# Second quartic factor of a Newton step: two matmuls of 128 columns for m and y against one of 256 columns on a joined tile

## The chip, the core and the metric

The kernel runs on one core of one Trainium2 chip. The metric is the device time of one execution in microseconds (us). A core has five engines that run side by side, each with its own queue of instructions: TensorE (PE in the profile, its weight loads PEld), VectorE (DVE), ScalarE (ACT), GpSimd (POOL) and SyncE (SP, which only issues DMA transfers here). They wait for each other through semaphores. Matmul results land in PSUM, which the kernel uses as eight banks of 128 x 512 f32; everything else lives in SBUF or in DRAM.

## The reference

The input x is 32 batches of 32 channels of 128 x 128, f32. Two layers follow, each a residual on a group normalisation.

```
# layer 0: x = x + sqrtm(_gn(x))
normA = sqrt(sum(A2 * A2));  Y = A2 / normA;  Z = I
for _ in range(5):
    T = 0.5 * (3 I - Z @ Y);  Y = Y @ T;  Z = T @ Z
sA = Y * sqrt(normA)

# layer 1: x = x + spectral_conv(_gn(x))
x_dht = real(fft2(x))
top = einsum('bixy,ioxy->boxy', x_dht[:, :, :32, :32], weights1)
bot = einsum('bixy,ioxy->boxy', x_dht[:, :, -32:, :32], weights2)
y = real(ifft2(zeros with top and bot put in their corners))
```

Layer 0 is the heavy one: for each of 1024 channels, five coupled Newton-Schulz steps on a 128 x 128 matrix. Layer 1 keeps 64 x 32 frequencies of each channel, mixes the channels there and transforms back.

## The kernel before

A group is four channels (tiles of 128 x 4 x 128, one PSUM bank). Layer 0 of a group is the generator newton (L400). It folds the five Newton steps into two quartic factors and a last product. quartic (L364) makes v from mb and m, then w from the transpose of v plus r, then q from v and w. With the first q, newton makes y = q m / MS (L404) and the next m = MS q y (L406), both copied out of PSUM by ScalarE through taken (L271, the copy is L276). The transpose of m gives mb (L408) and r (L409). With the second q, L412 makes two products: pw = q m and py = q y. pw is copied as one 128 x 512 to a tile called "t" (L413, name w in the code); py is copied channel by channel, scaled by that channel's norm sn (L416, tile "y4"). products(w, q) (L418) follows, then products(t, y) is added to the input (L420).

products (L304) takes one PSUM bank and issues four matmuls of 128 columns, one per channel. All matmuls of layer 0 have L307 in the profile; their tiles tell them apart: "m,q" is pw, "y,q" is both py and the product of L406, "q,t" is products(w, q). The transposes are L313. In profile names a group's m in the first quartic is "x".

Batches 1 to 18 are "far": for them v's transpose goes by VectorE and two DMAs on SyncE's queue through DRAM (L373 to L386), and GpSimd adds r (L388). The other batches ("near") transpose on TensorE.

The order of work is written by hand as lanes (L997 on). Up to nine groups are in progress. In each round every lane runs one step; each yield from rest ends two steps, so the parts of a group lie two rounds apart, and other groups' instructions stand between them in each queue. A new group starts every three (far) or five (near) rounds. The same loop weaves in layer 1: folding on GpSimd (L433), forward transforms (L455, L461, L467), spectra (L523), channel mixing (wide_products L608, small_products L678, last_products L723), and the inverse (L859, L881, with copies at L893 and unfolding at L898 and L827). The tile framework then places the semaphores and may move an instruction within its engine's queue; DMAs and some activations are pinned to program order (kept).

Rooms (L259) says how many places each kind of tile has: the first number in a pool that stays, the second in a pool that is freed when the early stage ends. y and m have (4, 2) each. In the tail, weights (L747) loads the last channel-mixing weights on SyncE's queue into rooms that Newton no longer needs: kinds lists which kind may be taken after how many steps of the last group.

Of the kernel before, what the change touches and what calls it, by code (L numbers as in the profile page):

```python
# [29 lines left out]
F32 = mybir.dt.float32  # L30
# [6 lines left out]
P = 128  # L37
# [13 lines left out]
MS = -QA * QS  # L51
# [17 lines left out]
def conv_preact_kernel(  # L69
# [8 lines left out]
    nc = tc.nc  # L78
# [24 lines left out]
    for i, n in enumerate(GROUPS):  # L103
        few = n <= NB
        shape = [KK // 2, P, n, 64] if few else [KK, P, B, 32]
# [5 lines left out]
        shape = [KK, 4, 32, 8 * C] if few else [KK, 4, B, L * C]  # L111
# [7 lines left out]
    sets = ctx.enter_context(tc.tile_pool(name="sets", bufs=1))  # L119
# [4 lines left out]
    first = ExitStack()  # L124
    early = first.enter_context(tc.tile_pool(name="early", bufs=1, side="right"))
# [21 lines left out]
    def bank():  # L147
        return ps8.tile([P, 4, P], F32, tag="ps", name="ps")
# [107 lines left out]
        yield  # L256


    rooms = dict(b=(4, 2), xt=(10, 4), x=(3, 2), r=(5, 2), v=(3, 3), w=(3, 2), q=(4, 2), y=(4, 2))  # L259
    rooms.update(m=(4, 2), mb=(2, 1), t=(3, 2), y4=(2, 2), turn=(0, 4))  # L260
    turns = dict.fromkeys(rooms, 0)

    def four(tag, more):
        n, m = rooms[tag]
        if more:
            turns[tag] += 1
            if turns[tag] % (n + m) >= n:
                return early.tile([P, 4, P], F32, tag=tag + "_early", name=tag, bufs=m)
        return sets.tile([P, 4, P], F32, tag=tag, name=tag, bufs=n)

    def taken(ps, tag, more, f=1.0):  # L271
        t = four(tag, more)
        if f == 1.0:
            nc.scalar.copy(t, ps)
        else:
            nc.scalar.mul(t, ps, f)  # L276
        return t

    def plus(ps, f, t, tag, more):

        s = four(tag, more)
        nc.vector.scalar_tensor_tensor(s, ps, f, t, ALU.mult, ALU.add)  # L282
        return s
# [6 lines left out]
    def plus_eye(mb, far, more):  # L290

        r = four("r", more)
        if far:
            nc.gpsimd.tensor_tensor(
                blocks(r).rearrange("p a c j -> p c a j"),
                mb.rearrange("p c (a j) -> p c a j", a=4),
                eye.rearrange("p c (a j) -> p c a j", a=4),
                ALU.add,
            )
        else:  # L300
            nc.gpsimd.tensor_tensor(r, mb, eye, ALU.add)  # L301
        return r

    def products(lhsT, rhs):  # L304
        ps = bank()
        for j in range(4):
            nc.tensor.matmul(ps[:, j, :], lhsT[:, j], rhs[:, j], start=True, stop=True)  # L307
        return ps

    def transposed(t):  # L310
        ps = bank()
        for j in range(4):
            nc.tensor.transpose(ps[:, j, :], t[:, j, :], ident)  # L313
        return ps
# [49 lines left out]
    def quartic(m, mb, r, far, more, wide):  # L364


        v = plus(products(mb, m), -1 / (QA * QR * QS), m, "v", more)
        if far:


            t = four("turn", more)
            form = "p c (b i) -> p b c i" if wide else "p c (i b) -> p b c i"
            nc.vector.transpose(blocks(t), v.rearrange(form, b=4))  # L373
            held = dram.tile([P, 512], F32, name="turn", tag="turn", bufs=8)
            kept(nc.sync.dma_start(out=held, in_=t.rearrange("p c x -> p (c x)")))
            yield from rest
            w = four("w", more)
            wb = blocks(w).rearrange("p a c j -> p a (c j)")
            if wide:
                for b in range(4):  # L380
                    rows = slice(32 * b, 32 * b + 32)
                    src = held[:, P * b : P * b + P].rearrange("(a i) x -> i a x", a=4)
                    kept(nc.sync.dma_start(out=wb[rows], in_=src))
            else:
                src = held.rearrange("(a i) (b x) -> (i b) a x", a=4, b=4)
                kept(nc.sync.dma_start(out=wb, in_=src))  # L386
            yield from rest
            nc.gpsimd.tensor_tensor(w, w, r, ALU.add)  # L388
            w = blocks(w).rearrange("p a c j -> p c a j")
        else:  # L390
            yield from rest
            w = plus(transposed(v), 1.0, r, "w", more)
        yield from rest
        q = plus(products(v, w), 1 / (16 * QS * QS), eye, "q", more)
        yield from rest
        return q
# [3 lines left out]
    def newton(g, sn, xt, m, mb, r, far, more):  # L400


        q = yield from quartic(m, mb, r, far, more, False)
        y = taken(products(q, m), "y", more, 1 / MS)  # L404
        yield from rest
        m = taken(products(q, y), "m", more, MS)  # L406
        yield from rest
        mb = taken(transposed(m), "mb", more, QR * QS / MS)  # L408
        r = plus_eye(mb, far, more)  # L409
        yield from rest  # L410
        q = yield from quartic(m, mb, r, far, more, True)
        pw, py = products(q, m), products(q, y)  # L412
        w, y = taken(pw, "t", more, 1 / MS), four("y4", more)  # L413
        for j in range(4):
            c = 4 * g + j
            nc.scalar.mul(y[:, j, :], py[:, j, :], sn[:, c : c + 1])  # L416
        yield from rest
        t = plus(products(w, q), -0.5 * EYE / 1.5, eye, "t", more)  # L418
        yield from rest
        nc.vector.tensor_tensor(xt, products(t, y), xt, ALU.add)  # L420
        yield

    folds = {}
    settled = []
# [322 lines left out]
    def weights():  # L747


        kinds = [("b", 2)] * 3 + [("x", 2), ("b", 4), ("x", 4), ("x", 10), ("y", 10), ("y", 10)]  # L750
        kinds += [("m", 11)] * 2 + [("r", 12)] * 4 + [("mb", 15)] * 2 + [("v", 15)] * 2
        kinds += [("w", 16)] * 2 + [("y", 16), ("m", 16), ("r", 17)] + [("q", 19)] * 3
        first = B * C // 4 - 10
        for half in range(4, 2 * KK):
            while True:
                if kinds and kinds[0][1] <= len(steps_of_last):
                    kind = kinds.pop(0)[0]
                    break
                if len(settled) > first and settled[first] < rounds - 4:
                    kind = "xt"  # L760
                    first += 1
                    break
                yield
            t = four(kind, False)
            late_wts.append(t)
            kept(
                nc.sync.dma_start(
                    out=t, in_=wk[half // 2, :, half % 2].rearrange("p q t o -> p q (t o)")
                )
            )  # L770
            yield
# [157 lines left out]
    rounds = 0  # L929
# [67 lines left out]
    while todo or any(lanes) or posts or specs or prods or backs:  # L997
# [3 lines left out]
        for i in range(LANES):  # L1001
# [5 lines left out]
            if lanes[i] is None and todo and room and rounds >= due:  # L1007
                due = max(due, rounds - 1) + (FAR if far else NEAR)
                while norms:
                    step(norms)  # L1010
                b, g = todo.pop(0)
                xt = ready[0][0]
                lanes[i] = (b, g, xt, newton(g, made[b][3], *ready.pop(0), far, has_more(b, g)))
                if stages:
                    stage()
                if not todo:
                    loads.append(weights())
            if lanes[i] is not None:
                b, g, xt, steps = lanes[i]
# [80 lines left out]
```

## Time and profile before

| what | value |
|---|---|
| time, median of 3 runs | 3108.08 us (3098.29 to 3114.35) |
| profiled execution, span from first to last instruction | 3098.6 us |
| profiled execution's own time beside its span | not listed apart; the quickest run is 3098.29 us |
| TensorE / weight loads busy | 2948.7 / 2828.6 us |
| VectorE / ScalarE / GpSimd busy | 2340.0 / 1704.0 / 1998.0 us |
| mean granted TensorE clock | 0.983 |
| ScalarE: L276 t, y, m, mb (128 x 512) x256 each | 595, 596, 604, 597 ns |
| ScalarE: L416 y4 (128 x 128) x1024 | 367 ns |
| ScalarE: copies of 128 x 256 at L893, L477 | 375, 379 ns |

The profile's groups give, for each line and form, how many instructions there were, their busy time together (overlaps counted once), the mean length of one, and the engine's idle time just before them with what ended it. For TensorE the mean length contains the pipeline, so the distance between starts says more than the length. In "128*128 128x256" the first pair is the rows and columns of the array in use, the second the partitions and elements written.

### The profile page before, as it was taken

How to read it: one execution, taken by the hardware profiler on the slowest of the kernel's cores; microseconds unless marked ns; L12 is line 12 of the kernel's file. 1: busy time of each engine (PE TensorE's matmuls, PEld its weight loads, DVE VectorE, ACT ScalarE, POOL GpSimd, SP SyncE). 2: the span in 40 equal slices, each digit the busy share in tenths (PEclk: the TensorE clock that was granted, in tenths of full speed). 3: DMA queues.
4: the chain of work that ended last, by engine and by line, in shares of the span. 5: the costliest groups of instructions: out<-in, count | busy, mean ns of one | idle time of the engine just before them, and what ended most of it. 6: DMA issues, size and time to landing. Idle time of an engine off the chain costs nothing. (4 is left out here: it accounts for less than half of the span.)

```text
span 3098.6 us, 79471 instructions
## 1 busy us (share of the span) xinstructions
PE 2948.7 (95%) x29760; PEld 2828.6 (91%) x29760; DVE 2340.0 (76%) x5178; ACT 1704.0 (55%) x4153; POOL 1998.0 (64%) x2312
## 2 busy tenths in 40 slices
PE   6999999999999999999999999999999998999994
PEld 6899999999999999999999998998899988899983
DVE  6788887888888787788877555788778766878654
ACT  3566556666665665666654444555454544555552
POOL 3567677677776666677665434768677764777453
PEclk9999999999999999999999999999999999999996
DMA  4576676666666666676743466667676876766666
GB/s 130 164 216 207 202 217 211 210 213 214 212 209 208 209 207 183 201 212 208 219 146 100 143 217 214 226 228 235 206 250 209 269 233 211 236 208 204 194 218 221
DMA packets 475150, 636.78 MB, mean 206 GB/s; under 512 B 97040, under 2 KB 255248, under 8 KB 474768
## 3 DMA queue, kind: packets, MB, share of 16 engines
q1 hardware_dynamic: 361872, 425.88, 42.8%
q10 hardware_dynamic: 112896, 205.83, 21.7%
q8 instruction: 237, 3.88, 0.5%
q14 instruction: 145, 1.19, 0.1%
HBM read 402.42 MB, written 229.11 MB: 204 GB/s over the span
## 5 line engine op out<-in xcount | busy, mean ns | idle before, releaser
L388 POOL TENSOR_TENSOR w<-w,r 128x512 f32<-128x512 f32 x288 | 366.3, 1276 | 324.3 <-DMA w<-turn 274.8
L307 PE MATMUL ps<-w,v 128*128 128x128 f32 x4096 | 554.6, 279 | 18.0 <-DVE w L282 7.7
L341 ACT ACTIVATE b<-b,a_off,a_scr 128x128 f32<-128x128 f32 x1024 | 468.7, 490 | 154.6 <-issue 48.1
L307 PE MATMUL ps<-y,q 128*128 128x128 f32 x4096 | 527.0, 277 | 6.2 <-ACT d L893 2.1
L307 PEld LDWEIGHTS ps<-w,v 128*128 128x128 f32 x4096 | 504.0, 194 | 25.1 <-POOL w L388 11.0
L307 PEld LDWEIGHTS ps<-y,q 128*128 128x128 f32 x4096 | 490.5, 193 | 9.6 <-issue 2.6
L433 POOL TENSOR_TENSOR fold<-xt 128x256 f32<-128x256 f32 x512 | 363.8, 731 | 204.5 <-DVE xt L420 192.2
L282 DVE SCALAR_TENSOR_TENSOR q<-ps,eye 128x512 f32<-128x512 f32 x512 | 348.0, 680 | 156.8 <-PE ps L307 151.5
L827 POOL TENSOR_TENSOR yt<-yt,d 128x512 f32<-128x512 f32 x248 | 311.2, 1282 | 153.7 <-ACT d L893 116.0
L301 POOL TENSOR_TENSOR r<-mb,eye 128x512 f32<-128x512 f32 x112 | 142.7, 1274 | 311.3 <-ACT mb L276 298.8
L348 POOL TENSOR_SCALAR x<-xt,a_nm,a_sc 128x128 f32<-128x128 f32 x736 | 322.7, 451 | 19.5 <-DVE a_n L231 19.5
L416 ACT ACTIVATE y<-ps,a_t_s 128x128 f32<-128x128 f32 x1024 | 291.4, 367 | 58.1 <-PE ps L307 57.6
L202 DVE BATCH_NORM_STATS2 a_st<-xs 128x6 f32<-128x128 f32 x1024 | 229.2, 278 | 108.7 <-DMA xs<-in_xt 107.9
L307 PE MATMUL ps<-m,q 128*128 128x128 f32 x2048 | 276.4, 278 | 8.1 <-DVE q L282 5.2
L307 PE MATMUL ps<-x,b 128*128 128x128 f32 x2048 | 277.0, 279 | 6.8 <-POOL x L348 5.6
L307 PE MATMUL ps<-m,mb 128*128 128x128 f32 x2048 | 276.7, 279 | 6.6 <-ACT d L893 4.3
L307 PE MATMUL ps<-x,q 128*128 128x128 f32 x2048 | 277.8, 279 | 3.3 <-DVE q L282 1.6
L307 PE MATMUL ps<-y,t 128*128 128x128 f32 x2048 | 275.1, 277 | 2.1 <-DVE t L282 2.0
L276 ACT ACTIVATE t<-ps 128x512 f32<-128x512 f32 x256 | 152.3, 595 | 223.1 <-PE ps L307 214.4
L307 PE MATMUL ps<-q,t 128*128 128x128 f32 x2048 | 274.9, 278 | 0.0
L373 DVE STREAM_TRANSPOSE turn<-v 128x512 f32<-128x512 f32 x288 | 262.0, 910 | 4.6
L307 PEld LDWEIGHTS ps<-m,q 128*128 128x128 f32 x2048 | 251.6, 193 | 10.7 <-DVE q L282 5.8
(148 smaller groups left out, 5768.2 us busy)
## 6 DMA issues: line engine op xcount, KB each, us to landing
turn<-turn SPq DMA_DIRECT2D x288, 256.0 KB
b<-in_x ACTq DMA_DIRECT2D x256, 256.0 KB
xt<-in_xt ACTq DMA_DIRECT2D x256, 256.0 KB
xs<-in_xt ACTq DMA_DIRECT2D x256, 256.0 KB
mid<-xt SPq DMA_DIRECT2D x256, 256.0 KB
yt<-mid SPq DMA_DIRECT2D x128, 512.0 KB
out<-yt SPq DMA_DIRECT2D x120, 512.0 KB
w<-turn SPq DMA_DIRECT2D x144, 256.0 KB
```

What stands on the lines that cost most here:

```text
L202: nc.vector.bn_stats(st[:, 4 * i + c, :], tiles[i][:, c, :])
L276: nc.scalar.mul(t, ps, f)
L282: nc.vector.scalar_tensor_tensor(s, ps, f, t, ALU.mult, ALU.add)
L301: nc.gpsimd.tensor_tensor(r, mb, eye, ALU.add)
L307: nc.tensor.matmul(ps[:, j, :], lhsT[:, j], rhs[:, j], start=True, stop=True)
L341: nc.scalar.activation(t, x, AF.Identity, bias=offset[:, c], scale=scale[:, c])
L348: nc.gpsimd.tensor_scalar(m[:, j, :], xt[:, j, :], nm[:, c // 2 : c // 2 + 1], sc[:, c : c + 1], ALU.add, ALU.mult,)
L373: nc.vector.transpose(blocks(t), v.rearrange(form, b=4))
L388: nc.gpsimd.tensor_tensor(w, w, r, ALU.add)
L416: nc.scalar.mul(y[:, j, :], py[:, j, :], sn[:, c : c + 1])
L433: nc.gpsimd.tensor_tensor(f[:, :, 64 * half : 64 * half + 64], xt[:, :, 0:64], xt[:, :, 64:128], op)
L827: engine.tensor_tensor(yh, yh, d, op)
```

## The change

y and m of the second half of a Newton step share one tile of the new kind "my", 128 x 4 x 2 x 128: for each channel y first, then m. The copies of L404 and L406 write into the two halves. The two products of L412 become four matmuls of 256 columns, one per channel with q as the stationary side, into two PSUM banks: each bank holds two channels, each with q y beside q m. The copy of w is made in two parts, one per bank, and the scaled copies of y read from both banks. "my" has (4, 2) places of double size in place of those of y and m. In weights the two halves of a "my" tile take two loads; the list of kinds is changed to suit.

```diff
-    rooms = dict(b=(4, 2), xt=(10, 4), x=(3, 2), r=(5, 2), v=(3, 3), w=(3, 2), q=(4, 2), y=(4, 2))
-    rooms.update(m=(4, 2), mb=(2, 1), t=(3, 2), y4=(2, 2), turn=(0, 4))
+    rooms = dict(b=(4, 2), xt=(10, 4), x=(3, 2), r=(5, 2), v=(3, 3), w=(3, 2), q=(4, 2))
+    rooms.update(my=(4, 2), mb=(2, 1), t=(3, 2), y4=(2, 2), turn=(0, 4))
...
+        shape = [P, 4, 2, P] if tag == "my" else [P, 4, P]
...
-        y = taken(products(q, m), "y", more, 1 / MS)
+        ym = four("my", more)
+        y, ym_m = ym[:, :, 0, :], ym[:, :, 1, :]
+        nc.scalar.mul(y, products(q, m), 1 / MS)
         yield from rest
-        m = taken(products(q, y), "m", more, MS)
+        m = ym_m
+        nc.scalar.mul(m, products(q, y), MS)
...
-        pw, py = products(q, m), products(q, y)
-        w, y = taken(pw, "t", more, 1 / MS), four("y4", more)
+        both = [bank().rearrange("p (j k) x -> p j k x", k=2) for _ in range(2)]
+        for j in range(4):
+            nc.tensor.matmul(both[j // 2][:, j % 2], q[:, j], ym[:, j], start=True, stop=True)
+        w, y = four("t", more), four("y4", more)
+        for h in range(2):
+            nc.scalar.mul(w[:, 2 * h : 2 * h + 2, :], both[h][:, :, 1, :], 1 / MS)
         for j in range(4):
             c = 4 * g + j
-            nc.scalar.mul(y[:, j, :], py[:, j, :], sn[:, c : c + 1])
+            nc.scalar.mul(y[:, j, :], both[j // 2][:, j % 2, 0, :], sn[:, c : c + 1])
...
-        kinds = [("b", 2)] * 3 + [("x", 2), ("b", 4), ("x", 4), ("x", 10), ("y", 10), ("y", 10)]
-        kinds += [("m", 11)] * 2 + [("r", 12)] * 4 + [("mb", 15)] * 2 + [("v", 15)] * 2
-        kinds += [("w", 16)] * 2 + [("y", 16), ("m", 16), ("r", 17)] + [("q", 19)] * 3
+        kinds = [("b", 2)] * 3 + [("x", 2), ("b", 4), ("x", 4), ("x", 10)]
+        kinds += [("my", 11)] * 2 + [("r", 12)] * 4 + [("mb", 15)] * 2 + [("v", 15)] * 2
+        kinds += [("w", 16)] * 2 + [("my", 16), ("r", 17)] + [("q", 19)] * 3
...
+                spare.extend([t] if len(t.shape) == 3 else [t[:, :, k, :] for k in range(2)])
+            t = spare.pop(0)
```

More of the change, by code (lines that the diff above doesn't have):

```diff
@@ L267, in four @@
             if turns[tag] % (n + m) >= n:
-                return early.tile([P, 4, P], F32, tag=tag + "_early", name=tag, bufs=m)
-        return sets.tile([P, 4, P], F32, tag=tag, name=tag, bufs=n)
+                return early.tile(shape, F32, tag=tag + "_early", name=tag, bufs=m)
+        return sets.tile(shape, F32, tag=tag, name=tag, bufs=n)
     def taken(ps, tag, more, f=1.0):
@@ L747, in weights @@
     def weights():
-        kinds = [("b", 2)] * 3 + [("x", 2), ("b", 4), ("x", 4), ("x", 10), ("y", 10), ("y", 10)]
-        kinds += [("m", 11)] * 2 + [("r", 12)] * 4 + [("mb", 15)] * 2 + [("v", 15)] * 2
-        kinds += [("w", 16)] * 2 + [("y", 16), ("m", 16), ("r", 17)] + [("q", 19)] * 3
+        kinds = [("b", 2)] * 3 + [("x", 2), ("b", 4), ("x", 4), ("x", 10)]
+        kinds += [("my", 11)] * 2 + [("r", 12)] * 4 + [("mb", 15)] * 2 + [("v", 15)] * 2
+        kinds += [("w", 16)] * 2 + [("my", 16), ("r", 17)] + [("q", 19)] * 3
         first = B * C // 4 - 10
+        spare = []
         for half in range(4, 2 * KK):
-            while True:
+            while not spare:
                 if kinds and kinds[0][1] <= len(steps_of_last):
[L757 to L760, printed above, removed]
+                    t = four(kinds.pop(0)[0], False)
+                elif len(settled) > first and settled[first] < rounds - 4:
+                    t = four("xt", False)
                     first += 1
-                    break
-                yield
-            t = four(kind, False)
+                else:
+                    yield
+                    continue
+                spare.extend([t] if len(t.shape) == 3 else [t[:, :, k, :] for k in range(2)])
+            t = spare.pop(0)
             late_wts.append(t)
```

## The prediction

> **What bounds the kernel now.** I read the page's busy shares and its forty slices first, then the windows by stage, then the groups of TensorE by form, then single stretches of the timeline, and the waits last.
>
> The page, busy time by engine and the slices of PE:
>
> ```profile
> PE 2948.7 (95%) x29760; PEld 2828.6 (91%) x29760; DVE 2340.0 (76%) x5178; ACT 1704.0 (55%) x4153; POOL 1998.0 (64%) x2312
> ...
> PE   6999999999999999999999999999999998999994
> ```
>
> TensorE is busy in all but the two ends; ScalarE has 45% to spare. "Busy" can hide waiting, so the windows, chosen by stage (columns: length, then busy us and count of PE, PEld, DVE, ACT, POOL, granted clock, DMA share, GB/s):
>
> ```profile
> 50.00:300.00 250.00, 243.54 (x2169) 236.56 (x2168) 196.36 (x446) 148.27 (x366) 163.42 (x191) 0.99 0.60 185
> 300.00:1500.00 1200.00, 1186.43 (x10670) 1152.72 (x10669) 985.07 (x2204) 729.18 (x1803) 842.62 (x933) 0.99 0.68 209
> 1500.00:1750.00 250.00, 248.00 (x2243) 240.81 (x2242) 183.07 (x431) 131.20 (x321) 148.41 (x187) 0.99 0.42 130
> 1750.00:1910.00 160.00, 155.38 (x2077) 142.63 (x2076) 84.72 (x204) 75.61 (x171) 64.22 (x88) 1.00 0.72 225
> 1910.00:2500.00 590.00, 568.74 (x5602) 541.92 (x5600) 466.16 (x987) 312.17 (x783) 426.33 (x499) 0.99 0.69 227
> 2500.00:2940.00 440.00, 412.63 (x5646) 391.46 (x5645) 311.50 (x638) 230.95 (x539) 268.68 (x322) 0.98 0.68 216
> ```
>
> From 50 to 1750 us PE is busy 97 to 99%; from 1750 to 2940 us 94 to 97%. Counting the blocks of the second-quartic product by their start in the trace, 163 of the 256 groups of four channels fall before 1750 us and 93 after. So the pitch of TensorE's instructions sets the time, and a microsecond off PE is nearly a microsecond off the end.
>
> The TensorE groups by form (count, busy, mean ns of one; the mean is a pipelined length, not the pitch):
>
> ```profile
> L307 PE MATMUL ps<-y,q 128*128 128x128 f32 x4096 | 527.0, 277 | 6.2 <-ACT d L893 2.1 <-ACT y L276 2.0 <-DVE q L282 1.1
> ...
> L307 PE MATMUL ps<-m,q 128*128 128x128 f32 x2048 | 276.4, 278 | 8.1 <-DVE q L282 5.2 <-DVE w L282 2.2 <-DVE yt L898 0.6
> ...
> L523 PE MATMUL ps<-u,tab 64*64 64x256 f32 x512 | 35.9, 397 | 0.0
> ```
>
> The form "m,q" is products(q, m) of the second quartic, four matmuls in each of 256 groups: 1024 matmuls, but 2048 records. Every f32 matmul of this kind is two records, each with a weight load ("y,q" has two calls per group). Pitches come from the timeline (start, length, engine, line, operation, tiles, count):
>
> ```profile
> 1502.43 1.06 PE L307 MATMUL ps<-m,q 128*128 128x128 f32 x8
> 1503.32 1.06 PE L307 MATMUL ps<-y,q 128*128 128x128 f32 x8
> 1504.21 1.06 PE L307 MATMUL ps<-w,v 128*128 128x128 f32 x8
> ```
>
> ```profile
> 359.17 1.09 PE L523 MATMUL ps<-u,tab 64*64 64x256 f32 x16
> ```
>
> Eight records of 128 columns start 0.89 us before the next eight: 111.7 ns a record (in the whole trace 112 or 111 ns is by far the commonest distance). L523 is the only form with 256 columns and no wait inside: its 16 records are four sets of four that run side by side, and in the trace the sets start 216 ns apart (584, 800, 1016 ns). At L881, 256 columns are again 216 ns and 252 columns 212.
>
> [...]the weight loads follow each other at the matmuls' 112 ns, and PEld's 91% lies under PE's 95%. [...]
>
> **The change part by part.**
>
> *TensorE, the matmuls.* Out go 2048 matmuls of 128 columns (the four of pw and four of py, 256 groups), in come 1024 of 256 columns. In records: 4096 x 111.7 = 457.4 us against 2048 x 216 = 442.4 us, 15.0 us less. The streamed columns are the same[...]. [...] I take 216. Nearly all of it is on the path: the 163 groups before 1750 us give 9.6 us in full; for the 93 later ones (5.4 us) I count three quarters, 4.1, since PE waits there for others now and then. Sum 13.7 us. In the order of the built program PE's instructions are otherwise the same as before, except for one swapped matmul.
>
> *ScalarE, the evacuation of w.* One 128x512 of 595 ns becomes two 128x256; rows L893 and L477 show 375 and 379 ns for that size. 256 x (2 x 377 - 595) = 41 us more on ScalarE, 1704 to 1745, 56% of the span. Hidden under PE; without that cover 41 us.
>
> *When w is whole.* Before, w's four matmuls end first, and its copy ends 1.69 us after the block starts (median of the trace). After, bank 0 is done at 0.86 and bank 1 at 1.73 us, plus the 0.2 us that the copy lags behind now. In 165-odd groups of the built order ScalarE runs w01, y0, y1, w23, y2, y3: w01 ends at 1.45, w23 at 1.07 + 0.38 + 2 x 0.37 + 0.38 = 2.57 us, 0.88 us later. In some 75 groups both w come first: 2.31. Who waits is products(w, q) on PE, with all its queue behind it. Its start stands 4.55 us (median), 2.7 us (a tenth) after the copy's end in the trace; were all copies 0.9 us later, the shortfalls would sum to 1.8 us in 5 groups. The second half is needed only 0.45 us after the first, so less: I take 1 us, bounds 0 and 2.3 (at 1.0 us).
>
> *y4's copies* end at about 3.3 us against 3.2 (median): nothing; their reader starts 5 us or more later in 95% of groups.
>
> *PSUM.* Bank 0 is held until y1, 2.2 us against 1.7; bank 1 to 3.3, 2.4 from its own start. Matching each block with the last reader of its bank before it, PE takes banks 4.2 us (median) after they come free, under 1.5 us in 5%: half a microsecond later costs under 1 us. I take none, the bound is 1.
>
> *The joined tile.* y and m are written, and m is read by VectorE and PE, in runs of 128 elements with gaps; the moving data of one channel are 256 elements in a row. The folded copies at L433 and L477 are strided too and cost no more than their neighbours of one size: nothing. m's room now opens when y is made, one step sooner, but y's room already had four places then: nothing.
>
> *The tail's weights.* Four of SyncE's 28 late loads go into halves of a "my" tile, two of them one step later (a round is about 2 us there), in pieces of 512 bytes. They were issued from 3011.4 to 3013.7 us and L723 first reads at 3048.4; the loads behind them on SP move with them. No wait of L723 on a DMA is in the profile. Nothing; without that cover about 2 us.
>
> Sum: -13.7 + 1 = -12.7 us. The profiled execution shows its span, 3098.6 us, and the quickest run listed is 3098.29, so nothing visible lies around it; 3098.6 becomes 3085.9. The median of the runs, 3108.1, is 9.5 us above that execution, and I carry the difference over: 3095.4, 0.41% less.
>
> The waits that speak for this (waiting engine, its releaser: us, times, longest):
>
> ```profile
> ACT t L276 <- PE ps L307: 214.4, 171, 4.1
> ...
> PE ps L307 <- ACT t L276: 0.9, 1, 0.9
> ```
>
> ScalarE waits for PE before w 171 times, PE for w's copy once in the run.
>
> **The rivals.** [...]stalls go with it: 20.5 us, less 1: about 3089. For it: L461's 512 columns come at 427 ns often[...]. Against it: 216 and 212 at L523 and L881. *The gain doesn't come through*: the wide matmul pays as much as two, or the other engines' chains set the pace after all: 3107. For it: 94% windows; against it: the 97 to 99% ones. *Slower: w's second half behind its neighbours on ScalarE.* Between w01 and w23 stand y's copies, and sometimes the 490 ns activations of L341; if w23 comes later than I count, PE stops at products(w, q). From the same distances: copies 2.5 us later cost 19 us (21 groups), 3.0 us later 35 us (43 groups), 3.5 us 63. It breaks even against 13.7 us at about 2.2 us, and ends slower from there; at 3.0 us it is 3108 - 14 + 35 = 3129. My count is 0.9 us, so ScalarE would have to run two further microseconds late as a rule.
>
> **How the numbers follow.** Forecast 0.67, the bigger gain 0.13, no gain 0.13, slower 0.07. Range: 3108 - 20.5 = 3087.6, and some 2 us for the runs' own spread, gives 3085.5; up to no gain at 3108.5. The slower case stays out. A measurement of this kernel can tell about 0.5% (15.5 us) from no change; the forecast lies just inside. Faster by more: all of the bigger gain and a quarter of the forecast's own chance (a pitch nearer 214, or the runs' spread), 0.13 + 0.17 = 0.30; same 0.50 + 0.13 = 0.63; slower 0.07.
>
> **What would show it.** Right: a form of 256 columns, 2048 records at 215 to 217 ns, PE's busy time near 2935, ScalarE near 1745, PE's wait on t's copy under 3 us. The pitch is wrong if 223 or 213 ns stands there; the cover is wrong if PE waits for t by tens of microseconds; the late stages are wrong if the saving stops at 1750 us.

## The result and the profile after

The changed kernel takes 3085.1 us (median of 6 runs, 3077.3 to 3097.8); the kernel before, measured again beside it, 3104.2 us (6 runs, 3098.3 to 3114.4). The ratio is 0.9938, 95% interval 0.9919 to 0.9956: 19.1 us less, 13.7 to 25.1. The profiled execution has a span of 3088.1 us and took 3090.2, so about 2 us lie around a span.

The page after, busy time and the slices of PE:

```profile
PE 2938.3 (95%) x27712; PEld 2755.2 (89%) x27712; DVE 2335.0 (76%) x5178; ACT 1721.5 (56%) x4409; POOL 2001.5 (65%) x2312
...
PE   6999999999999999999999999999999988999994
```

2048 records are gone from TensorE (29760 to 27712), and from the weight loads as many. Busy PE falls by 10.4 us, weight loads by 73.4, and the time by 19.1: at least 54 of the 73 us of load time that vanished don't show in it. Of PE's busy time, stretches in which the granted clock was 0.5 cost 35.4 us in the trace of before and 40.7 in this one (estimated as half of the busy time inside them); without them PE's work falls from 2913.4 to 2897.7 us, by 15.7.

The new form among the groups of TensorE, and the block in the timeline (start, length, engine, line, operation, tiles, count):

```profile
L418 PE MATMUL ps<-my,q 128*128 128x256 f32 x2048 | 494.7, 385 | 12.3 <-DVE q L283 5.9 <-DVE w L283 2.8 <-ACT d L903 2.5
```

```profile
800.43 1.89 PE L418 MATMUL ps<-my,q 128*128 128x256 f32 x8
802.16 1.05 PE L308 MATMUL ps<-my,q 128*128 128x128 f32 x8
803.05 1.06 PE L308 MATMUL ps<-y,t 128*128 128x128 f32 x8
```

Eight wide records take 802.16 - 800.43 = 1.73 us, 216 ns each; eight of 128 columns still take 0.89. Over all 2048 records the median distance to the next start is 216 ns (5th to 90th percentile: 215 to 218). The busy time of L418, 494.7 us, is more than 442 mostly because the modelled end of each block lies 0.16 us after the start of the next one (1.89 against 1.73), which makes some 41 us in 256 groups.

The two largest stages in the windows, with the same columns as before:

```profile
300.00:1500.00 1200.00, 1189.31 (x9844) 1130.13 (x9843) 994.70 (x2230) 744.98 (x1941) 853.44 (x942) 1.00 0.69 211
...
1910.00:2500.00 590.00, 572.84 (x5289) 533.92 (x5288) 466.58 (x993) 316.91 (x834) 432.43 (x503) 0.99 0.69 228
```

PE is as full as before (99 and 97%), so it is still the bound. The waits for w's copy, seen from ScalarE and from PE (two views; us, times, longest):

```profile
ACT t L421 <- PE ps L418: 235.1, 213, 4.3
```

```profile
PE ps L308 <- ACT t L421: 1.8, 2, 1.4
```

Before, these were 214.4 and 0.9 us. PE waits for w twice in the run.

### The profile page after: what moved, and what is told of

Same layout as the page of the kernel before. It is cut to its first block, busy times and chain, and to the rows that moved or that the text cites. A ratio compares the mean times of both kernels' runs of the same rounds, so it can differ in the third digit from the quotient of the medians.

```text
span 3088.1 us, 75794 instructions
## 1 busy us (share of the span) xinstructions
PE 2938.3 (95%) x27712; PEld 2755.2 (89%) x27712; DVE 2335.0 (76%) x5178; ACT 1721.5 (56%) x4409; POOL 2001.5 (65%) x2312
## 5 line engine op out<-in xcount | busy, mean ns | idle before, releaser
L418 PE MATMUL ps<-my,q 128*128 128x256 f32 x2048 | 494.7, 385 | 12.3 <-DVE q L283 5.9
L418 PEld LDWEIGHTS ps<-my,q 128*128 128x128 f32 x2048 | 373.4, 192 | 56.9 <-DVE q L283 6.5
L421 ACT ACTIVATE t<-ps 128x256 f32<-128x256 f32 x512 | 191.4, 382 | 242.3 <-PE ps L418 235.1
L424 ACT ACTIVATE y<-ps,a_t_s 128x128 f32<-128x128 f32 x1024 | 311.0, 370 | 0.0
L308 PE MATMUL ps<-my,mb 128*128 128x128 f32 x2048 | 276.4, 278 | 5.4 <-ACT d L903 3.8
L308 PE MATMUL ps<-my,q 128*128 128x128 f32 x2048 | 276.0, 278 | 3.4 <-ACT my L407 2.3
L308 PEld LDWEIGHTS ps<-my,q 128*128 128x128 f32 x2048 | 260.3, 193 | 13.2 <-ACT my L407 2.9
```

Of the source, the lines that this page charges most:

```text
L418: nc.tensor.matmul(both[j // 2][:, j % 2], q[:, j], ym[:, j], start=True, stop=True)
L421: nc.scalar.mul(w[:, 2 * h : 2 * h + 2, :], both[h][:, :, 1, :], 1 / MS)
L424: nc.scalar.mul(y[:, j, :], both[j // 2][:, j % 2, 0, :], sn[:, c : c + 1])
```

## The experiments

All kernels but one group of controls are edits of the changed kernel. Differences are given in us against the kernel before in the same session (ratio less one, times its median); in brackets the 95% interval. A single run of one kernel scatters by some 6 us (standard deviation), so profiles of one execution each can't settle a few us: in the first profile pair the two kernels differ by 10.5 us, and all of that arises between groups 80 and 120, where the profiled execution of before happened to stall.

### The changed kernel, three more times

Unchanged (a1, c4), and with the channels of each bank issued in the order 1, 0, 3, 2 (d3):

```diff
-        for j in range(4):
+        for j in (1, 0, 3, 2):
             nc.tensor.matmul(both[j // 2][:, j % 2], q[:, j], ym[:, j], start=True, stop=True)
```

> The changed kernel once more, for a firmer difference. Theory A (the pitch: 2048 wide records of 216 ns in place of 4096 of 111.7 ns, and nothing else that matters): 15 us less than before, ratio 0.995. Theory B (the pitch, and beyond it a gain of some 4 to 5 us from elsewhere: another evacuation, fewer stalls, fewer half-clock windows): 19 to 20 us less, 0.9937. Theory C (my forecast's discounts were right, the first measurement was lucky): 12 to 13 us less, 0.996.

> The changed kernel a third time, to tell 15 us (the pitch alone) from 19 us (pitch and something more): theory A says the mean of the three measurements moves towards 15, theory B that it stays at 19.

> The changed kernel with the two channels of each bank in the other order: the same work, waits and banks. Theory A: the same as the changed kernel, 19 us below before by its three measurements (15 if these were lucky). Theory S: anything from 13 to 23 below.

Measured: a1 0.9939 (0.9923 to 0.9954), 19.0 us less; c4 0.9943 (0.9922 to 0.9964), 17.7 less; d3 0.9938 (0.9917 to 0.9958), 19.3 less. With the first measurement (19.1) that makes four, all at 18 to 19 us. Theory C (12 to 13) is below a1's interval (14.3 to 23.9), but not below c4's (11.2 to 24.2); the 15.0 us of the pitch lie inside all four intervals, in their smaller half. Taken as four independent measurements they give 18.8 us, 16.0 to 21.7 (an estimate), which speaks for B; the next section shows that sessions differ by more than such an interval says, so between A and B these runs don't decide.

### The width alone undone

```diff
-            nc.tensor.matmul(both[j // 2][:, j % 2], q[:, j], ym[:, j], start=True, stop=True)
+            for k in range(2):
+                nc.tensor.matmul(
+                    both[j // 2][:, j % 2, k], q[:, j], ym[:, j, k], start=True, stop=True
+                )
```

> Joined tile, both banks with y and m side by side, copies of w in two halves as in the changed kernel, but each wide matmul is again two of 128 columns with q loaded twice. Theory A: all of the gain is gone, within 2 us of before. Theory B: 4 to 5 us of the gain stay, if it is the evacuation or the layout that gives them. Theory C: 1 us slower than before, for the later w.

> The joined tile and banks with two matmuls of 128 columns, a second time: this differs from the changed kernel by nothing but the matmuls' width. Pitch alone: within 2 us of before. If its first measurement was lucky or unlucky by the scatter: 3 to 4 us off, and then the width is worth 15 to 16 or 22 us.

The block of the second one in the timeline:

```profile
799.99 1.95 PE L419 MATMUL ps<-my,q 128*128 128x128 f32 x16
801.78 1.06 PE L308 MATMUL ps<-my,q 128*128 128x128 f32 x8
```

Sixteen records in 1.79 us, 112 ns each. Measured: 1.0002 (0.9988 to 1.0016) and, in another session, 0.9974 (0.9959 to 0.9990): 0.6 us more and 8.1 us less. One and the same program: two measurements 9 us apart, with intervals that barely touch. So an interval within one session seems to understate the spread. Weighted by runs (14 and 7) the narrow kernel is some 2.5 us below before, and the width is worth about 16 of the 18 to 19 us, 10 to 19 by the choice of session. Theory A fits the first measurement; the second lies outside of all that was expected for it (2 us, or 3 to 4), and taken alone it would leave 8 us to tile and copies. The mean of the two shows no gain of more than 4 us from these.

### Where the gain arises: far and near groups alone

```diff
+        if far:
+            both = [bank().rearrange("p (j k) x -> p j k x", k=2) for _ in range(2)]
...
+        else:
+            pw, py = products(q, m), products(q, y)
+            w, y = taken(pw, "t", more, 1 / MS), four("y4", more)
...
```

In a4 and b1, which are one kernel, the condition is "not far".

> The wide matmul in the 144 far groups alone; the 112 near ones use the two products of before on the joined tile. Theory A: 144 x 8 x 7.33 ns = 8.4 us less than before. Theory C (far counts in full, near three quarters): 8.4 us too. Rival D (in the far stage rounds are paced by transfers, so that PE's time comes back as waiting): 0 to 3 us less.

> The wide matmul in the 112 near groups alone. Theory A: 112 x 8 x 7.33 ns = 6.6 us less than before. Theory C: about 5 us less. Rival D (the gain arises late, where PE waits, and waits shrink with it): more than 10 us less.

> The wide matmul in the 112 near groups alone, once more, because its first measurement (14.9 us less) is twice its share of the pitch (6.6 us). Theory A (pitch alone): 6 to 8 us less than before. Theory B (in the near stages a saved microsecond is worth more than one[...]): 12 to 15 us less again.

Measured: far alone 0.9969 (0.9955 to 0.9982), 9.6 us less; near alone 0.9952 (0.9937 to 0.9967), 14.9 less, and again 0.9966 (0.9954 to 0.9978), 10.6 less. The far share fits the pitch (8.4). D falls: the far stage is not paced by rounds or transfers. The near share is larger than its part of the pitch (6.6) by both measurements, and the three quarters of my forecast (about 5) is below both intervals (10.2 to 19.6 and 6.8 to 14.3). The two shares together, 20 to 25 us, are more than the whole change brings: the surplus of the near-only kernel is as large as the scatter between sessions above.

### The joined tile alone

```diff
-        both = [bank().rearrange("p (j k) x -> p j k x", k=2) for _ in range(2)]
...
+        pw, py = products(q, m), products(q, y)
+        w, y = taken(pw, "t", more, 1 / MS), four("y4", more)
```

> The joined tile alone: y and m lie side by side, but the two products, their banks and the copies are those of before in all groups. If the tile costs and brings nothing, as forecast: within 2 us of before. If part of what the near-only and the far-only kernel gained beyond their share of the pitch comes from the tile or its places: 3 to 5 us less than before.

Measured: 1.0009 (0.9999 to 1.0020), 2.8 us more. No gain from the tile is seen; it explains none of the near-only kernel's surplus.

### What a microsecond of TensorE is worth: added

```diff
         for j in range(4):
-            nc.tensor.matmul(both[j // 2][:, j % 2], q[:, j], ym[:, j], start=True, stop=True)
+            for _ in range(2 if not far and j == 0 else 1):
+                nc.tensor.matmul(
+                    both[j // 2][:, j % 2], q[:, j], ym[:, j], start=True, stop=True
+                )
```

For the far groups the condition is "far".

> The changed kernel, and in each of the 112 near groups the first wide matmul is issued twice (the second writes the same values): 2 records of 216 ns, 48.4 us of TensorE in all. Against the changed kernel (19 us below before): if all of it is on the path (A), 48 us more, so 29 us above before; if three quarters count, as my forecast had it for the late stages, 36 more, 17 above before; if a near microsecond counts double (B), 80 or more.

> The same in the 144 far groups: 144 x 2 x 216 ns = 62.2 us of TensorE. If all of it is on the path (A and my forecast alike): 62 us more than the changed kernel, 43 above before. If transfers or rounds pace the far stage (D): under 30 us more.

Measured: near 1.0079 (1.0055 to 1.0104), 24.5 us above before, so 43.5 above the changed kernel (taken at 19.0 below): 0.90 of the 48.4 added. Far 1.0122 (1.0101 to 1.0144), 37.9 above before, 56.9 above the changed kernel: 0.91 of 62.2. Near and far are alike, which speaks against D. With the interval near is 0.74 to 1.06, so three quarters is just possible there; a double price is not. (The changed kernel was not measured in that session; its own uncertainty comes on top.)

### What a microsecond of TensorE is worth: taken away

```diff
-        for j in range(4):
+        less = not far
+        for j in range(0, 4, 2 if less else 1):
             nc.tensor.matmul(both[j // 2][:, j % 2], q[:, j], ym[:, j], start=True, stop=True)
...
+            pw = both[h][:, 0:1, 1, :].to_broadcast([P, 2, P]) if less else both[h][:, :, 1, :]
...
+            py = both[j // 2][:, 0 if less else j % 2, 0, :]
```

For the far groups, "less" is "far".

> The changed kernel, with the wide matmuls of the second and fourth channel left out in the 112 near groups (the copies read the first and third channel's results in their place, so half of that product is not computed there): 4 records of 216 ns a group, 96.8 us of TensorE less. If a microsecond of TensorE is worth one (A): 97 us below the changed kernel, 116 below before. If three quarters, as my forecast had it for the late stages: 73 below the changed kernel. If 0.9, as the added matmuls showed: 87. If more than one since stalls shrink too (B): over 105.

> The same left out in the 144 far groups: 124.4 us of TensorE less. A: 124 us below the changed kernel, 143 below before. If VectorE (82% busy there) or the transfers take over as the bound: 60 to 100 below the changed kernel.

Measured: near 0.9798 (0.9783 to 0.9814), 62.7 us below before, 45 below the changed kernel of the same session: 0.46 of 96.8. Far 0.9772 (0.9751 to 0.9794), 70.7 below before, 53 below the changed kernel: 0.43 of 124.4. Every share that was expected is higher. B falls for large steps: taking away a hundred microseconds brings less than half. The rest comes back as waiting. PE stands idle for 184 us (near) and 199 us (far) in these two traces, against 150 in the mean of the changed kernel's four, and the mean clock of their runs is 0.978 and 0.980 against 0.984. The largest single wait that grew, first with the far work left out, then in the changed kernel:

```profile
PE ps L308 <- POOL w L389: 27.0, 23, 4.2
```

```profile
PE ps L308 <- POOL w L389: 6.7, 4, 4.2
```

PE comes to products(v, w) before GpSimd has added r to w (which had to travel through DRAM). That is 20 of the 48 us of new idle time in the far case; the others are spread over many waits, and in the near case no single one stands out. PE is the bound of the kernel before by a narrow margin: the first 15 us are to be had nearly whole, the next hundred by half.

### The order of ScalarE's copies

```diff
         for h in range(2):
-            nc.scalar.mul(w[:, 2 * h : 2 * h + 2, :], both[h][:, :, 1, :], 1 / MS)
-        for j in range(4):
-            c = 4 * g + j
-            nc.scalar.mul(y[:, j, :], both[j // 2][:, j % 2, 0, :], sn[:, c : c + 1])
+            kept(nc.scalar.mul(w[:, 2 * h : 2 * h + 2, :], both[h][:, :, 1, :], 1 / MS))
+            for j in (2 * h, 2 * h + 1):
+                c = 4 * g + j
+                kept(nc.scalar.mul(y[:, j, :], both[h][:, j % 2, 0, :], sn[:, c : c + 1]))
```

This is f1, bank by bank. In d4 the two copies of w stand first and are pinned (kept) ahead of the four of y; in b4 the four of y are pinned ahead of the two of w. In the changed kernel the framework's own order has w01, y0, y1, w23, y2, y3 in 169 groups of its trace and both w first in 74, 66 of them far (the expectation below says 64).

> The changed kernel with ScalarE's copies held in the order y0, y1, y2, y3, w01, w23: w whole at about 3.43 us after the block starts in place of 2.57, its first half at 3.05 in place of 1.45. By the distances in the trace of before (a copy 1.3 to 1.5 us later cost 4.0 to 5.6 us) 4 to 6 us more than the changed kernel, about 14 below before. If w's copy has no price at all: 19 below before, as the changed kernel. If my rival was right that w's lateness is dear: slower than before.

> The changed kernel with ScalarE's copies held in the order w01, w23, y0, y1, y2, y3: w whole at 2.31 in place of 2.57 us, ScalarE waits for the second bank before it copies y. Theory A: within 1 us of the changed kernel. If w's lateness costs something at all: 1 to 2 us faster than the changed kernel, the best version of all.

> The changed kernel with ScalarE's copies pinned bank by bank: w01, y0, y1, w23, y2, y3. If the kernel with both w first lost 9 us because ScalarE stands waiting for the second bank with y behind it, this one is as fast as the changed kernel (18 to 19 us below before) or up to 3 us faster, since 64 of the far groups have both w first there. If pinning itself cost the 9 us: about 9 us below before again.

Measured: w last 0.9947 (0.9928 to 0.9967), 16.5 us less than before; w first 0.9971 (0.9961 to 0.9981), 9.0 less; bank by bank 0.9944 (0.9924 to 0.9963), 17.4 less. The order with w *first* is the one that loses, which nothing expected: some 9 us against the changed kernel, with an interval that lies clear of d3's in the same session. Pinning by itself shows no cost. With w last the price is 2 or 3 us, which the intervals don't tell from nothing; in its trace PE waits for w's copy a little more often than in the changed kernel (1.8 us, twice):

```profile
PE ps L308 <- ACT t L424: 5.0, 4, 2.4
```

The copies of w and y among ScalarE's groups (busy, mean ns, idle before them), w first and then bank by bank:

```profile
L424 ACT ACTIVATE y<-ps,a_t_s 128x128 f32<-128x128 f32 x1024 | 290.5, 374 | 0.0
L421 ACT ACTIVATE t<-ps 128x256 f32<-128x256 f32 x512 | 189.3, 381 | 300.8 <-PE ps L418 288.3 <-PE ps L308 5.2 <-DMA xs<-in_xt 4.8
```

```profile
L424 ACT ACTIVATE y<-ps,a_t_s 128x128 f32<-128x128 f32 x1024 | 318.0, 368 | 0.0
L421 ACT ACTIVATE t<-ps 128x256 f32<-128x256 f32 x512 | 196.0, 383 | 211.6 <-PE ps L418 203.9 <-PE ps L308 6.7
```

With w first ScalarE stands 301 us before w's copies, since the second one waits for the second bank while y0 and y1 of the first bank, ready long since, are queued behind it; bank by bank it stands 212 us. In the trace the six copies end 3.70 us after the block's start (mean of the near groups) against 3.28. PE does not wait long for w or y4, so if this is what costs 9 us, it acts through what ScalarE does next or through the release of both banks. That link is argued and not shown: PE is idle for 158 us in the trace of w first and for 147 to 156 in the four of the changed kernel, and bank by bank is no faster than the changed kernel, though it takes w first away from 74 groups.

### Programs that do the same work

Two edits of the kernel before that leave TensorE's records as they are, d1 and d2:

```diff
-        pw, py = products(q, m), products(q, y)
+        py, pw = products(q, y), products(q, m)
```

```diff
-        w, y = taken(pw, "t", more, 1 / MS), four("y4", more)
+        w, y = four("t", more), four("y4", more)
+        for h in range(2):
+            nc.scalar.mul(w[:, 2 * h : 2 * h + 2, :], pw[:, 2 * h : 2 * h + 2, :], 1 / MS)
```

> The kernel before with its two products in the other order (py, then pw): TensorE's records are the same in number and pitch, w is whole some 0.9 us later. Theory A with exact accounting: 0 to 2 us slower than before (a copy 0.9 us later costs 1.8 us by the distances in the trace). Theory S (programs that do the same work scatter by 3 to 5 us through where stalls fall): it may lie 3 to 5 us off in either direction.

> The kernel before with w copied in two halves of 128x256 from its one bank: ScalarE works 41 us more, nothing else changes. Theory A: within 1 us of before. Theory S: up to 3 to 5 us off. Theory E (the halved copy brings a part of the gain, as its first half is ready sooner): 3 to 5 us faster than before.

Measured: py first 1.0017 (1.0000 to 1.0035), 5.3 us more; w in halves 0.9990 (0.9979 to 1.0000), 3.1 less. With the joined tile alone (2.8 more) and the narrow kernel (0 and 8 less), programs with the same records on TensorE were measured from 8 below to 5 above before. That fits S, though A (0 to 2 us, and within 1 us) lies inside both intervals too. Either way a rest of 3 or 4 us can't be given a cause in this kernel by such runs. E (the halved copy brings a part) fits d2 but isn't told from S or A.

## Why the prediction was right and wrong, step by step

**The direction and the mechanism were right.** TensorE sets the time, and each pair of records loses 7.3 ns when it becomes one: 2 x 111.7 ns in the trace of before, the mean distance of starts inside the blocks, against 216. The pitch of 216 ns, taken from L523's sets, stands in the trace of the changed kernel. PE's busy time counted without what the half clock costs it is 2897.7 to 2900.8 us in the four traces of the wide kernel (the first, a1, c4, d3) and 2912.2 to 2914.2 in the six with matmuls of 128 columns in their place (before, a2, f2, c1, d1, d2): 13.8 us less in the mean, close to the 15.0 of the forecast. With the width alone undone, all of the gain is gone in one session and about half in the other. Whether the 7.3 ns belong to the stream or to the weight load that went with each record, no run here separates.

**The step that failed first is the base and its spread.** I carried over 9.5 us from the profiled execution to the median of three runs, 3108.1, and gave the range "some 2 us for the runs' own spread". The three runs shown already lay 16 us apart; with six runs the median was 3104.2, and in the later sessions 3102.3 to 3107.4, with a standard deviation of 4.6 to 6.9 us for one run. That is 3.9 of the 10.3 us between forecast and result. The result fell 0.4 us below the range; with 3104.2 as the base the same working would have put it inside.

**The other 6.4 us: the gain was larger than the sum, -12.7 us forecast, -19.1 measured.** The terms of the sum, one by one:

- "For the 93 later ones I count three quarters", and the early ones in full: added work costs 0.90 of its length near and 0.91 far. So the late groups were priced too low and the early ones too high, and the two errors cancel: 15.0 us at 0.91 is 13.6, where I had 13.7. The total of this term was right by luck. PE's idle 3 to 6% in the late windows was no measure of how much of its busy time is off the path.
- "I take 1 us" for w's lateness: PE's wait for w's copy rose from 0.9 to 1.8 us in the profiled executions, so the size fits, though the working doesn't. The copy of w ends 2.31 us after the block's start (median of the trace, and in the kernel that is pinned bank by bank), where I had 2.57: ScalarE's small copies overlap (L424: 311.0 us busy for 1024, 0.30 us each, not the 0.37 of the mean length that I added up). ScalarE's load was over-counted too: 1721.5, not 1745, since neighbouring copies overlap.
- What is left has no term in the sum: about 4 us beyond the 15.0 of the pitch, 6 beyond the -12.7, in four measurements of the wide kernel. By the mean granted clock of the runs, 0.9829 before and 0.9840 after, at most 3100 x 0.0011 = 3.4 us of it is less time at the half clock (see below); that is an account, not a cause. PE's idle time doesn't show it either: 150 us in the mean of the four wide traces, 151 in the six others. Programs with equal work on TensorE differ as much, so it stays open whether the surplus belongs to the change. So does that of the near-only kernel: 4 to 8 us beyond its pitch.

**The rivals.** The slower one had the wrong sign of the order: it feared w23 behind y's copies, and that order is as fast as any; the dear order is the opposite one, w first, where ScalarE waits for a bank with ready work behind it. "The gain doesn't come through" is excluded by every measurement of the wide kernel. The bigger gain leaned on L461, whose 512 columns often come at 427 ns: at half of that, 213.5 ns, 2048 records would save 20.2 us, near the 20.5 that it names. It came close in size, but not through such a pitch, since 216 was measured, and not through fewer stalls as far as PE's idle time shows.

**The covers held.** Joined tile: nothing, or 2.8 us within the scatter. PE's wait for w: 1.8 us, under the 3 of the forecast. PE busy 2938 against 2935, with 5 us more lost to the half clock than in the trace of before.

## What to carry to other kernels

Two matmuls with the same stationary side made into one saved 7.3 ns of 223 here, far less than the 36 ns of busy weight load that fell away with it (73.4 us over 2048 pairs, while the whole run gained 19.1): read the pitch of both widths from starts in the timeline, not from busy time or mean length. TensorE, 95% busy here, gave back nearly the full time for the first 15 us and less than half for a hundred: add and take away work of known length to see how far such a margin goes. ScalarE kept the pinned order of its copies in all 256 groups, and there the copies of what was finished first, bank by bank, did better than the copy that was wanted first; why, is not shown. And a forecast of an absolute time needs more than three runs of the kernel before, when single runs lie 16 us apart.

## What was not expected: TensorE's half clock

In the traces of before and after the granted clock is either 1 or 0.5. The stretches at half, 16 and 18 of them, last 3.41, 6.83 or 13.65 us, but for the last one of each trace (22.1 and 22.0). Windows of 3.4 us in the trace of before around one of them (length, PE, PEld, DVE, ACT and POOL busy, granted clock, DMA share, GB/s):

```profile
1194.50:1197.90 3.40, 3.36 (x32) 2.95 (x34) 3.40 (x3) 0.24 (x2) 2.44 (x2) 1.00 0.00 0
1197.90:1201.30 3.40, 1.69 (x20) 1.18 (x12) 3.33 (x11) 3.40 (x10) 0.00 (x0) 1.00 0.85 269
1201.30:1204.70 3.40, 1.40 (x7) 1.40 (x8) 1.02 (x3) 2.19 (x6) 2.76 (x3) 0.52 0.70 213
1204.70:1208.10 3.40, 3.40 (x18) 3.40 (x18) 0.69 (x1) 0.99 (x3) 3.40 (x6) 0.50 0.43 135
1208.10:1211.50 3.40, 3.40 (x32) 3.40 (x31) 0.69 (x1) 1.74 (x6) 2.25 (x2) 0.98 0.00 0
```

In the second window PE is busy for half, with a stall at its end; in the third and fourth the clock is 0.5, and the full fourth window holds 18 records in place of 32. In both traces the starts lie on one grid of 3.41 us (to 0.03 us). In the windows of this grid just before the 34 half-clock stretches PE was busy from 0 to 46%. Of the 1700 full-clock windows after the first 23 us that were followed by another none was under 44%; between 44% and 46% both happened. In the fullest window ahead of a stretch, the one shown here, PE was idle for 1.8 us (54% of 3.41). By this working, an estimate that no run tests, such a stall costs its own length, and up to 1.7 us more for each window at half clock (half of 3.41, as 18 records in place of 32 suggest). This may be a part of the scatter from run to run: within the runs of one kernel, time and time lost to the clock go together (correlation 0.5 to 0.8 in the samples of 14 runs and more), and from kernel to kernel the mean clock goes from 0.978 (near work left out, PE waits more) to 0.984.
